# Scores of 1024 users against 100,001 items on one core: chunks of 4096 items instead of 2048, with longer rows in stores and loads

## The chip, the cores and the metric

The kernel runs on one core of one Trainium2 chip. The metric is the device time of one execution in microseconds (us); medians of several runs are quoted. PE is TensorE, DVE is VectorE, ACT is ScalarE, POOL is GpSimd, and SP is SyncE, which issues the stores and loads treated here. The profile counts 16 DMA engines for the core. The chips that the runs fell on differ by some 5% of this kernel's time (before takes 1645 us on two and about 1733 us on another), all of it in the first third (the rest takes 1135.4 and 1136.0 us), for a reason that stays open (see the result), so kernels are compared on the same chip, as ratios, or from one common instruction of the trace to the end.

## The reference, cut to what matters

```python
e = emb[seq]                                   # 1024 x 50 gathered rows of 128 floats
prefix = jnp.cumsum(e, axis=1)
uF = prefix / denom[:, :, None]                # then normalised over the 1024 users
...
_, spikes = lax.scan(step, v0, x_seq)          # 50 time steps
uF_out = spikes.mean(axis=0)                   # 1024 x 128
scores = uF_out @ emb.T                        # 1024 x 100001 floats: 409.6 MB written
```

The first half (the gather phase) is 50 steps of gathers and small vector work. The second (the output stage) reads the table once (51 MB), multiplies, and writes 409.6 MB. The change concerns the second and the seam between the two.

## The kernel before: the parts concerned

Item rows are fetched in chunks of 2048, 16 chunks ahead. A partition holds every 128th row, so each piece of a load is one row of 512 bytes:

```python
CH = 2048; AHEAD = 16; HALF = 1024
r = rowp.tile([P, CH // P, D], F32, ...)
nc.sync.dma_start(out=r[:, :full, :],
                  in_=table[c0 : c0 + full * P, :].rearrange("(k p) d -> p k d", p=P))
```

A "preparation" makes 1024 items ready for the products: eight transposes into PSUM, then a split into an upper part (ACT) and a lower part (DVE).

```python
for k0 in range(0, hw, P):
    nc.tensor.transpose(pt[:, k0 : k0 + kw], r[:kw, (h0 + k0) // P, :], ident[:kw, :kw])
nc.scalar.copy(hi[:, :hw], pt[:, :hw])
nc.vector.tensor_tensor(lo[:, :hw], pt[:, :hw], hi[:, :hw].bitcast(F32), ALU.subtract)
```

The output stage goes chunk by chunk, and in a chunk through eight blocks of 128 users. A block is evicted from PSUM in pieces of 1024 columns, by DVE and ACT in turn, into one of four 1 MiB buffers, and stored. The next chunk is prepared along the way:

```python
op = ctx.enter_context(tc.tile_pool(name="o", bufs=4, reuse_waits="tile"))
for c0 in range(0, N, CH):
    for n in range(NB):                        # NB = 8
        o = op.tile([P, CH], F32, tag="o", ...)
        for h0 in range(0, w, HALF):
            ...                                # four products into po
            # DVE or ACT in turn: o[:, h0:h0+hw] = po * (1/T)
        nc.sync.dma_start(out=out[n * P : (n + 1) * P, c0 : c0 + w], in_=o[:, :w])
        if n in (1, 4) and c0:
            ... prepare(nxt, h0, ...)          # one of the two halves of the next chunk
        if n == 4 and c0 + AHEAD * CH < N:
            fetch(c0 + AHEAD * CH)
```

## Time and profile before

| before | value |
|---|---|
| time, median of the first 3 runs | 1730.06 us (1729.33 to 1733.63) |
| span of the profiled execution | 1642.6 us |
| DMA rate, loads mixed in / stores only | 395 / 406 GB/s |
| score stores | 1 MiB each, rows of 8192 bytes |
| loads | 1 MiB each, pieces of 512 bytes |

The profiled execution is 87 us shorter than the timed ones. Besides the lines that the prediction quotes, these of the page of before are needed below. The groups' columns are busy time and mean ns of one, then the idle time ahead of them and what ended it.

```profile
span 1642.6 us, 14074 instructions
...
DMA packets 98817, 488.20 MB, mean 297 GB/s; under 512 B 15845, under 2 KB 17592, under 8 KB 49592
...
L92 DVE TENSOR_TENSOR lo<-pt,hi 128x1024 fp32r<-128x1024 f32 x98 | 119.7, 1221 | 76.1 <-ACT hi L91 76.1
...
L91 ACT CAST hi<-pt 128x1024 fp32r<-128x1024 f32 x98 | 98.7, 1007 | 8.0 <-PE pt L90 8.0
```

The reader is to keep two durations: the halves of the split take 1221 ns on DVE and 1007 ns on ACT. A preparation therefore keeps the two evicting engines from evicting for about as long as one piece of a block (1223 ns on DVE, 1020 ns on ACT).

### The profile page before, as it was taken

What the parts mean: (1) busy time and instruction counts of PE and PEld (TensorE: products, weight loads), DVE (VectorE), ACT (ScalarE), POOL (GpSimd) and SP (SyncE); (2) the same over time, 40 slices, a digit from 0 to 9 for tenths busy, and PEclk for the clock granted to TensorE, in tenths of its full rate; (3) what the DMA queues carried; (4) which work ended last, traced back from release to release, by engine and by line L of the source; (5) the groups of instructions that cost most, each with busy time, mean ns of one, the idle gap of its engine ahead of it and who ended that gap; (6) DMA issues with size and microseconds to landing.
All of it is one profiled execution on the core that took longest, in us unless ns stands there. A gap on an engine that the chain in (4) does not pass through costs nothing.

```text
span 1642.6 us, 14074 instructions
## 1 busy us (share of the span) xinstructions
PE 1294.6 (79%) x4621; PEld 837.6 (51%) x4634; DVE 963.5 (59%) x1258; ACT 637.1 (39%) x698; POOL 378.4 (23%) x406
## 2 busy tenths in 40 slices
PE   5777777777777778778877877887788798888886
PEld 2332232223334556656655665565566566666664
DVE  4777777777776445444544544454455455555554
ACT  2332222323333344434443444444444444444443
POOL 7777777777771000000000000000000000000000
PEclk6555555555556899999999999999999999999999
DMA  9921222221223999999999999999999999999998
GB/s 256 257 53 53 53 53 53 53 53 53 53 53 142 396 397 393 404 394 386 398 399 391 391 404 393 392 396 400 391 393 401 394 417 409 404 406 406 401 402 347
DMA packets 98817, 488.20 MB, mean 297 GB/s; under 512 B 15845, under 2 KB 17592, under 8 KB 49592
## 3 DMA queue, kind: packets, MB, share of 16 engines
q1 hardware_dynamic: 85944, 461.07, 72.1%
q0 software_dynamic: 12800, 26.24, 6.1%
q8 instruction: 36, 0.59, 0.1%
q14 instruction: 37, 0.30, 0.1%
HBM read 77.65 MB, written 409.60 MB: 297 GB/s over the span
## 4 chain that ended last, share of the span: by engine, by line
DMA 54%; POOL 16%; PE 12%; issue 8%; DVE 5%; ACT 4%; DVEq 0%; ACTq 0%; SPq 0%; POOLq 0%
DMA scores<-o 51%; POOL e L122 16%; PE po L301 10%; ACT o L311 3%; DVE o L309 3%; DMA e<-in_L_rec_emb_table,idx 3%; PE pre L179 1%; PE pt L90 1%; PE pre L219 0%; DVE s L199 0%; DVE bs L229 0%; DVE uF L228 0%; ACT v L264 0%; DVE v L267 0%; PE count L189 0%
## 5 line engine op out<-in xcount | busy, mean ns | idle before, releaser
L301 PE MATMUL po<-hi,countR 128*128 128x512 f32 x1568 | 678.0, 432 | 183.8 <-ACT o L311 180.9
L309 DVE TENSOR_SCALAR o<-po 128x1024 f32<-128x1024 f32 x392 | 479.3, 1223 | 463.6 <-DMA scores<-o 438.9
L301 PE MATMUL po<-lo,countR 128*128 128x512 f32 x1568 | 645.8, 412 | 0.0
L311 ACT ACTIVATE o<-po 128x1024 f32<-128x1024 f32 (+1 forms) x392 | 399.9, 1020 | 633.0 <-DMA scores<-o 514.3
L301 PEld LDWEIGHTS po<-hi,countR 128*128 128x128 f32 x1568 | 314.1, 200 | 336.3 <-ACT o L311 249.6
L122 POOL DMA_INDIRECT e<-in_L_rec_emb_table,idx x400 | 377.7, 944 | 124.3 <-issue 115.5
L301 PEld LDWEIGHTS po<-lo,countR 128*128 128x128 f32 x1568 | 315.0, 201 | 60.0
L219 PE MATMUL pre<-ident,e 128*128 128x128 f32 x400 | 143.0, 443 | 122.8 <-DMA e<-in_L_rec_emb_table,idx 118.7
L179 PE MATMUL pre<-zT,l 50*128 50x512 f32 x200 | 186.8, 1086 | 2.3 <-DVE uF L228 2.3
L219 PEld LDWEIGHTS pre<-ident,e 128*128 128x128 f32 x400 | 80.3, 206 | 202.1 <-DMA e<-in_L_rec_emb_table,idx 179.4
L92 DVE TENSOR_TENSOR lo<-pt,hi 128x1024 fp32r<-128x1024 f32 x98 | 119.7, 1221 | 76.1 <-ACT hi L91 76.1
L237 ACT ACTIVATE r<-mv,eps 128x1 f32<-128x1 f32 x50 | 14.7, 295 | 296.7 <-DVE mv L233 296.7
L228 DVE SCALAR_TENSOR_TENSOR uF<-rlen,pre 128x512 f32<-128x512 f32 x100 | 68.3, 683 | 95.3 <-PE pre L219 95.3
L90 PE MATMUL pt<-ident,rows 128*128 128x128 f32 x782 | 108.3, 283 | 15.6 <-ACT o L311 9.9
L90 PEld LDWEIGHTS pt<-ident,rows 128*128 128x128 f32 x782 | 89.3, 144 | 47.5 <-ACT o L311 35.3
L91 ACT CAST hi<-pt 128x1024 fp32r<-128x1024 f32 x98 | 98.7, 1007 | 8.0 <-PE pt L90 8.0
L179 PEld LDWEIGHTS pre<-zT,l 50*128 50x128 f32 x200 | 57.4, 317 | 65.3 <-issue 38.4
L264 ACT ACTIVATE v<-uF,hgb,a 128x1024 f32<-128x1024 f32 (+1 forms) x51 | 60.8, 1193 | 49.4 <-DVE a L257 49.2
L229 DVE BATCH_NORM_STATS2 bs<-uF 128x6 f32<-128x512 f32 x100 | 69.5, 695 | 3.4
L267 DVE SCALAR_TENSOR_TENSOR v<-negv,v 128x1024 f32<-128x1024 f32 (+1 forms) x51 | 61.6, 1209 | 13.0 <-ACT v L264 13.0
L199 DVE TENSOR_SCALAR s<-v 128x1024 bf16<-128x1024 f32 (+1 forms) x51 | 60.9, 1194 | 0.1
L266 DVE TENSOR_TENSOR negv<-s,v 128x1024 f32<-128x1024 bf16 x48 | 58.1, 1211 | 0.0
(41 smaller groups left out, 216.8 us busy)
## 6 DMA issues: line engine op xcount, KB each, us to landing
scores<-o SPq DMA_DIRECT2D x384, 1024.0 KB, 9.0
scores<-o SPq DMA_DIRECT2D x8, 848.5 KB, 7.4
e<-in_L_rec_emb_table,idx POOLq DMA_INDIRECT x400, 2.5
rows<-in_L_rec_emb_table SPq DMA_DIRECT2D x1, 832.0 KB
rows<-in_L_rec_emb_table SPq DMA_DIRECT2D x48, 0.5 KB, 11.7
idx<-in_r_seq SPq DMA_DIRECT2D x1, 200.0 KB, 3.0
r<-in_L_rec_emb_table SPq DMA_DIRECT2D x1, 25.0 KB
rows<-in_L_rec_emb_table SPq DMA_DIRECT2D x1, 16.5 KB
```

The costliest lines, as they stand in the source:

```text
L90: nc.tensor.transpose(pt[:, k0 : k0 + kw], r[:kw, (h0 + k0) // P, :], ident[:kw, :kw])
L91: nc.scalar.copy(hi[:, :hw], pt[:, :hw])
L92: nc.vector.tensor_tensor(lo[:, :hw], pt[:, :hw], hi[:, :hw].bitcast(F32), ALU.subtract)
L122: nc.gpsimd.indirect_dma_start(out=es[t][:, n * P : (n + 1) * P], out_offset=None, in_=table, in_offset=bass.IndirectOffsetOnAxis(ap=idx[: ...
L179: nc.tensor.matmul(pre[h], lhsT=l, rhs=zT[:, h * BANK : (h + 1) * BANK], start=t == 0, stop=False, skip_group_check=True,)
L219: nc.tensor.matmul(pre[h][:, k : k + P], lhsT=e[:, h * BANK + k : h * BANK + k + P], rhs=ident, start=False, stop=last, is_transpose=True, ...
L228: nc.vector.scalar_tensor_tensor(uF[:, cs], rlen[:, cs], 1.0 / (t + 1), pre[h], ALU.max, ALU.mult)
L229: nc.vector.bn_stats(bs[:, h, :], uF[:, cs])
L267: nc.vector.scalar_tensor_tensor(vt[:, cs], negv[:, cs], -0.5, vt[:, cs], ALU.mult, ALU.add)
L301: nc.tensor.matmul(po[:, k0 : k0 + kw], lhsT=countR[:, n * P : (n + 1) * P], rhs=part[:, k0 : k0 + kw], start=j == 0, stop=j == 1,)
L309: nc.vector.tensor_scalar_mul(o[:, h0 : h0 + hw], po[:, :hw], 1.0 / T)
L311: nc.scalar.mul(o[:, h0 : h0 + hw], po[:, :hw], 1.0 / T)
```

## The change

Its intent: fewer and longer rows for the DMA engines, in both directions, and an earlier first store. The core of the diff:

```diff
-CH = 2048
-AHEAD = 16
+CH = 4096
+AHEAD = 7
...
+            nc.sync.dma_start(           # a load: eight table rows in a row per partition, 4 KB runs
+                out=r[:, : whole * KQ, :].rearrange("p (q k) d -> p q (k d)", q=whole),
+                in_=table[c0 : c0 + whole * HALF, :].rearrange("(q p k) d -> p q (k d)", p=P, k=KQ),
+            )
...
+        return (                         # the split reads PSUM with a stride, to undo that order
+            pt.rearrange("d (k p) -> d p k", k=KQ),
+            hi.rearrange("d (p k) -> d p k", k=KQ),
+            lo.rearrange("d (p k) -> d p k", k=KQ),
+        )
...
+        x(halves[0])                     # the last time step, in halves and reordered
+        x(halves[1])
+        ...                              # the first block: five stores of 256, 256, 512, 512, 512 KB
...
-    op = ctx.enter_context(tc.tile_pool(name="o", bufs=4, reuse_waits="tile"))
+    op = ctx.enter_context(tc.tile_pool(name="o", bufs=3, reuse_waits="tile"))
...
+                if n == NB - 1 and q < 2:
+                    ready(c + 1, 2 + q)  # preparations 2 and 3 of the next chunk, inside the last block
+            if c or n > 1:
+                store(n, c0, o[:, :w])   # 2 MiB, rows of 16 KB
+            if n in (2, 5):
+                ready(c + 1, n // 5)     # preparations 0 and 1
+        if c + AHEAD < len(chunks):
+            fetch(c + AHEAD, rowp)       # 2 MiB
```

(Comments are mine; cuts are marked with "...".)

More of the change, by code (lines that the diff above doesn't have):

```diff
@@ L23 @@
 V_TH = 1.0
-CH = 2048
-AHEAD = 16
+CH = 4096
+AHEAD = 7
 HALF = 1024
+KQ = HALF // P
 BANK = 512
@@ L50, in rec_kernel @@
     const = ctx.enter_context(tc.tile_pool(name="const", bufs=1))
-    embp = ctx.enter_context(tc.tile_pool(name="embT", bufs=4))
-    rowp = ctx.enter_context(tc.tile_pool(name="rows", bufs=AHEAD))
-    countR = const.tile([P, B], F32R, tag="countR", name="countR")
+    embp = ctx.enter_context(tc.tile_pool(name="embT", bufs=1))
+    rowp = ctx.enter_context(tc.tile_pool(name="rows", bufs=AHEAD - 1))
+    countA = const.tile([P, P], F32R, tag="countA", name="countA")
+    countB = const.tile([P, BANK - P], F32R, tag="countB", name="countB")
@@ L56, in rec_kernel @@
+    countC = const.tile([P, B - BANK], F32R, tag="countC", name="countC")
+    counts = [countA]
+    counts += [countB[:, k : k + P] for k in range(0, BANK - P, P)]
+    counts += [countC[:, k : k + P] for k in range(0, B - BANK, P)]
     ident = const.tile([P, P], F32, tag="ident", name="ident")
+    chunks = [(c0, min(CH, N - c0)) for c0 in range(0, N, CH)]
     rows = {}
     split = {}
-    def fetch(c0):
-        w = min(CH, N - c0)
-        full, rest = divmod(w, P)
-        r = rowp.tile([P, CH // P, D], F32, tag="rows", name=f"rows_{c0}")
+    order = {}
@@ new lines, in rec_kernel, with fetch @@
+    for c, (c0, w) in enumerate(chunks):
+        for q in range(-(-w // HALF)):
+            order[c, q] = len(order)
+    def fetch(c, pool):
+        c0, w = chunks[c]
+        r = pool.tile([P, CH // P, D], F32, tag="rows", name=f"rows_{c}")
+        whole = w // HALF
+        if whole:
+            nc.sync.dma_start(
+                out=r[:, : whole * KQ, :].rearrange("p (q k) d -> p q (k d)", q=whole),
+                in_=table[c0 : c0 + whole * HALF, :].rearrange("(q p k) d -> p q (k d)", p=P, k=KQ),
+            )
+        c1 = c0 + whole * HALF
+        full, rest = divmod(w - whole * HALF, P)
+        k0 = whole * KQ
@@ L66, in fetch @@
         if full:
             nc.sync.dma_start(
-                out=r[:, :full, :],
-                in_=table[c0 : c0 + full * P, :].rearrange("(k p) d -> p k d", p=P),
+                out=r[:, k0 : k0 + full, :],
+                in_=table[c1 : c1 + full * P, :].rearrange("(k p) d -> p k d", p=P),
             )
         if rest:
-            nc.sync.dma_start(out=r[:rest, full, :], in_=table[c0 + full * P : c0 + w, :])
-        rows[c0] = r
-    def prepare(c0, h0, pt):
-        w = min(CH, N - c0)
-        hw = min(HALF, w - h0)
-        r = rows[c0]
-        if c0 == 0 and h0 == 0:
-            nc.vector.memset(r[0:1, 0, :], 0.0)
-        hi = embp.tile([P, HALF], F32R, tag="hi", name=f"hi_{c0}_{h0}")
-        lo = embp.tile([P, HALF], F32R, tag="lo", name=f"lo_{c0}_{h0}")
+            nc.sync.dma_start(out=r[:rest, k0 + full, :], in_=table[c1 + full * P : c0 + w, :])
@@ new lines, in fetch, with turned, slot @@
+        rows[c] = r
+    def turned(c, q, pt):
+        hw = min(HALF, chunks[c][1] - q * HALF)
+        if c == 0 and q == 0:
+            nc.vector.memset(rows[c][0:1, 0, :], 0.0)
+        for k0 in range(0, hw, P):
+            kw = min(P, hw - k0)
+            nc.tensor.transpose(pt[:, k0 : k0 + kw], rows[c][:kw, q * KQ + k0 // P, :], ident[:kw, :kw])
+    def slot(c, q):
+        i = order[c, q] % 6
+        pool = embp if i < 4 else embp2
+        hi = pool.tile([P, HALF], F32R, tag=f"hi{i}", name=f"hi_{c}_{q}")
+        lo = pool.tile([P, HALF], F32R, tag=f"lo{i}", name=f"lo_{c}_{q}")
+        split[c, q] = hi, lo
+        return hi, lo
@@ L85, in prepare, with views, upper @@
+    def views(c, q, pt, hi, lo):
+        hw = min(HALF, chunks[c][1] - q * HALF)
+        if hw < HALF:
+            return pt[:, :hw], hi[:, :hw], lo[:, :hw]
+        return (
[3 more added lines that the diff above has]
+        )
+    def upper(c, q, pt):
+        hi, lo = slot(c, q)
+        hw = min(HALF, chunks[c][1] - q * HALF)
         if hw % 2:
@@ L87, in prepare, with lower, product, store @@
             nc.vector.memset(lo[:, hw : hw + 1].bitcast(F32), 0.0)
-        for k0 in range(0, hw, P):
-            kw = min(P, hw - k0)
-            nc.tensor.transpose(pt[:, k0 : k0 + kw], r[:kw, (h0 + k0) // P, :], ident[:kw, :kw])
-        nc.scalar.copy(hi[:, :hw], pt[:, :hw])
-        nc.vector.tensor_tensor(lo[:, :hw], pt[:, :hw], hi[:, :hw].bitcast(F32), ALU.subtract)
-        split[c0, h0] = hi, lo
+        vp, vh, vl = views(c, q, pt, hi, lo)
+        nc.scalar.copy(vh, vp)
+    def lower(c, q, pt):
+        vp, vh, vl = views(c, q, pt, *split[c, q])
+        nc.vector.tensor_tensor(vl, vp, vh.bitcast(F32), ALU.subtract)
+    def prepare(c, q, pt):
+        turned(c, q, pt)
+        upper(c, q, pt)
+        lower(c, q, pt)
+    def product(po, c, q, n, k0, kw):
+        kw += kw % 2
+        for j, part in enumerate(split[c, q]):
+            nc.tensor.matmul(
+                po[:, :kw],
+                lhsT=counts[n],
+                rhs=part[:, k0 : k0 + kw],
+                start=j == 0,
+                stop=j == 1,
+            )
+    def store(n, c0, o):
+        nc.sync.dma_start(out=out[n * P : (n + 1) * P, c0 : c0 + o.shape[1]], in_=o)
     with ExitStack() as ph:
+        row0p = ph.enter_context(tc.tile_pool(name="rows0", bufs=1))
         once = ph.enter_context(tc.tile_pool(name="once", bufs=1))
+        lp = ph.enter_context(tc.tile_pool(name="lif", bufs=2))
+        sp = ph.enter_context(tc.tile_pool(name="stats", bufs=3))
+        up = ph.enter_context(tc.tile_pool(name="uF", bufs=2))
         gp = ph.enter_context(tc.tile_pool(name="gather", bufs=3))
-        up = ph.enter_context(tc.tile_pool(name="uF", bufs=2))
-        sp = ph.enter_context(tc.tile_pool(name="stats", bufs=3))
-        lp = ph.enter_context(tc.tile_pool(name="lif", bufs=2))
         accp = ph.enter_context(tc.tile_pool(name="acc", bufs=1, space=bass.MemoryType.PSUM))
@@ L113, in rec_kernel @@
         nc.sync.dma_start(out=gb[:, 1:2], in_=beta.rearrange("(d o) -> d o", o=1))
-        for c0 in range(0, min(AHEAD * CH, N), CH):
-            fetch(c0)
+        for c in range(min(AHEAD, len(chunks))):
+            fetch(c, rowp if c else row0p)
         es = {}
@@ L169, in rec_kernel, with only @@
         count = [accp.tile([P, BANK], F32, tag=f"count{h}", name=f"count{h}") for h in range(B // BANK)]
-        def row0(t):
+        def only(t):
             l = sp.tile([T, D], F32, tag="l", name=f"l_{t}")
@@ L203, in rec_kernel @@
         v = s = None
-        correct(0, row0(0))
-        l = row0(1)
+        correct(0, only(0))
+        l = only(1)
         for t in range(T):
@@ L262, in rec_kernel, with x @@
             st = lp.tile([P, B], BF16, tag="s", name=f"s_{t}")
-            for h, cs in enumerate(halves if last else [whole]):
+            def x(cs):
                 nc.scalar.activation(vt[:, cs], uF[:, cs], AF.Identity, bias=hgb[:, 1:2], scale=a)
-                if t and not last:
-                    nc.vector.tensor_tensor(negv, s, v, ALU.subtract)
-                nc.vector.scalar_tensor_tensor(vt[:, cs], negv[:, cs], -0.5, vt[:, cs], ALU.mult, ALU.add)
-                if last:
-                    spike(st, vt, cs)
-                    counted(t, st, h)
-                    for k in range(0, BANK, P):
-                        put = nc.scalar.copy if k % (2 * P) == 0 else nc.vector.tensor_copy
-                        put(countR[:, h * BANK + k : h * BANK + k + P], count[h][:, k : k + P])
@@ L274, in rec_kernel, with step @@
-            v, s = vt, st
-            if t + 2 < T:
-                l = row0(t + 2)
-            if T - 10 <= t < T - 2 and t % 2 == 0:
-                k = (t - T + 10) // 2
-                prepare(k // 2 * CH, k % 2 * HALF, vp.tile([P, HALF], F32, tag="v1", name=f"pt_{k}"))
-    op = ctx.enter_context(tc.tile_pool(name="o", bufs=4, reuse_waits="tile"))
+            def step(cs):
+                nc.vector.scalar_tensor_tensor(vt[:, cs], negv[:, cs], -0.5, vt[:, cs], ALU.mult, ALU.add)
+            if not last:
+                x(whole)
+                if t:
+                    nc.vector.tensor_tensor(negv, s, v, ALU.subtract)
+                step(whole)
+                v, s = vt, st
+                if t + 2 < T:
+                    l = only(t + 2)
+                if T - 8 <= t < T - 2 and t % 2 == 0:
+                    q = (t - T + 8) // 2
+                    prepare(0, q, vp.tile([P, HALF], F32, tag="v1", name=f"pt_{q}"))
@@ new lines, in rec_kernel @@
+        pt = vp.tile([P, HALF], F32, tag="v0", name="pt_3")
+        turned(0, 3, pt)
+        x(halves[0])
+        x(halves[1])
+        for h, cs in enumerate(halves):
+            step(cs)
+            spike(st, vt, cs)
+            if h == 0:
+                counted(T - 1, st, 0)
+                nc.scalar.copy(countA, count[0][:, :P])
+        upper(0, 3, pt)
+        o = gp.tile([P, HALF], F32, tag="e", name="o_0_0_0")
+        for h, po in enumerate(pre):
+            product(po, 0, 0, 0, h * BANK, BANK)
@@ new lines, in rec_kernel @@
+        counted(T - 1, st, 1)
+        nc.scalar.mul(o[:, :BANK], pre[0], 1.0 / T)
+        store(0, 0, o[:, :BANK])
+        lower(0, 3, pt)
+        nc.vector.tensor_scalar_mul(o[:, BANK:], pre[1], 1.0 / T)
+        store(0, BANK, o[:, BANK:])
+        nc.scalar.copy(countB, count[0][:, P:])
+        for q in range(1, 4):
+            o = (up if q == 3 else gp).tile([P, HALF], F32, tag="uF" if q == 3 else "e", name=f"o_0_0_{q}")
+            po = vp.tile([P, HALF], F32, tag=f"v{q % 2}", name=f"po_0_0_{q}")
+            for k0 in range(0, HALF, BANK):
+                product(po[:, k0 : k0 + BANK], 0, q, 0, k0, BANK)
+            for h, cs in enumerate(halves):
+                if h == 0:
+                    nc.scalar.mul(o[:, cs], po[:, cs], 1.0 / T)
+                else:
+                    nc.vector.tensor_scalar_mul(o[:, cs], po[:, cs], 1.0 / T)
+            store(0, q * HALF, o)
+            if q == 1:
+                nc.vector.tensor_copy(countC, count[1])
@@ L285, in rec_kernel @@
+    embp2 = ctx.enter_context(tc.tile_pool(name="embT2", bufs=1, reuse_waits="tile"))
+    op = ctx.enter_context(tc.tile_pool(name="o", bufs=3, reuse_waits="tile"))
     psum = ctx.enter_context(
@@ L288, in rec_kernel, with ready @@
     turn = 0
-    for c0 in range(0, N, CH):
-        w = min(CH, N - c0)
+    def ready(c, q):
+        if (c, q) in order:
+            prepare(c, q, psum.tile([P, HALF], F32, tag="ps", name=f"pt_{c}_{q}"))
+    for c, (c0, w) in enumerate(chunks):
         for n in range(NB):
-            o = op.tile([P, CH], F32, tag="o", name=f"o_{c0}_{n}")
-            for h0 in range(0, w, HALF):
+            if c == 0 and n == 0:
+                continue
+            o = op.tile([P, CH], F32, tag="o", name=f"o_{c}_{n}")
+            for q in range(-(-w // HALF)):
+                h0 = q * HALF
                 hw = min(HALF, w - h0)
-                po = psum.tile([P, HALF], F32, tag="ps", name=f"po_{c0}_{n}_{h0}")
+                po = psum.tile([P, HALF], F32, tag="ps", name=f"po_{c}_{n}_{q}")
                 for k0 in range(0, hw, BANK):
-                    kw = min(BANK, hw - k0)
-                    kw += kw % 2
-                    for j, part in enumerate(split[c0, h0]):
-                        nc.tensor.matmul(
-                            po[:, k0 : k0 + kw],
-                            lhsT=countR[:, n * P : (n + 1) * P],
-                            rhs=part[:, k0 : k0 + kw],
-                            start=j == 0,
-                            stop=j == 1,
-                        )
+                    product(po[:, k0 : k0 + BANK], c, q, n, k0, min(BANK, hw - k0))
                 if turn % 2 == 0:
@@ L312, in rec_kernel @@
                 turn += 1
-            nc.sync.dma_start(out=out[n * P : (n + 1) * P, c0 : c0 + w], in_=o[:, :w])
-            nxt = c0 + CH
-            if n in (1, 4) and c0:
-                h0 = 0 if n == 1 else HALF
-                if nxt + h0 < N:
-                    prepare(nxt, h0, psum.tile([P, HALF], F32, tag="ps", name=f"pt_{nxt}_{h0}"))
-            if n == 4 and c0 + AHEAD * CH < N:
-                fetch(c0 + AHEAD * CH)
+                if c == 0 and n == 1 and q % 2:
+                    store(n, c0 + h0 - HALF, o[:, h0 - HALF : h0 + HALF])
+                if n == NB - 1 and q < 2:
[6 more added lines that the diff above has]
+            fetch(c + AHEAD, rowp)
 _INS = ["r_seq", "r_lengths", "L0_rec_emb_table", "L0_rec_gamma", "L0_rec_beta"]
```

## The prediction

> **What bounds the kernel now.** I read the page from the top: busy shares, then the 40 slices, then the chain of waits.
>
> ```profile
> PE 1294.6 (79%) x4621; PEld 837.6 (51%) x4634; DVE 963.5 (59%) x1258; ACT 637.1 (39%) x698; POOL 378.4 (23%) x406
> ...
> DMA  9921222221223999999999999999999999999998
> GB/s 256 257 53 53 53 53 53 53 53 53 53 53 142 396 397 393 404 394 386 398 399 391 391 404 393 392 396 400 391 393 401 394 417 409 404 406 406 401 402 347
> ...
> DMA 54%; POOL 16%; PE 12%; issue 8%; DVE 5%; ACT 4%; DVEq 0%; ACTq 0%; SPq 0%; POOLq 0%
> ```
>
> There are two programs in one. Up to about 505 us the GpSimd gathers pace the 50 time steps (400 issues of 0.94 us plus 0.3 us of issue each, about 1.24 us x 400 = 497 us). From 520 us to the end the DMA row stands at 9 and the rate at 390 to 417 GB/s: 409.6 MB of scores are written and two thirds of the table is read. The busiest compute engine, PE at 79% of the span, is not what ends the chain: 54% of it is DMA. The waits say the same from the other side, both evicting engines wait for a store to free its buffer:
>
> ```profile
> ACT o L311 <- DMA scores<-o: 514.3, 310, 5.9
> DVE o L309 <- DMA scores<-o: 438.9, 277, 5.7
> ```
>
> Next, the busy time of each engine in three stretches: with loads mixed in, stores only, and the tail. Columns after the times are PE clock, DMA share and GB/s.
>
> ```profile
> 740.21:1240.00 499.79, 398.56 (x1672) 301.11 (x1671) 252.11 (x209) 209.37 (x209) 0.00 (x0) 0.93 1.01 395
> 1320.00:1600.00 280.00, 248.32 (x1074) 174.43 (x1073) 161.72 (x134) 134.48 (x135) 0.00 (x0) 1.00 0.99 406
> ```
>
> The DMA engines are full in both (1.01 and 0.99). So only what shortens the DMA work itself, or starts it earlier, moves the end. The chain in order of time gives the cadence of that work:
>
> ```profile
> 740.21 16.93 DMA scores<-o x2
> 764.07 17.03 DMA scores<-o x2
> 788.02 17.01 DMA scores<-o x2
> ...
> 1576.67 8.97 DMA scores<-o
> 1587.05 8.97 DMA scores<-o
> 1597.43 8.98 DMA scores<-o
> ```
>
> With four buffers of 1 MiB the stores-only stretch comes round every 10.38 us, 2.595 us a store. With loads, eight stores and one 1 MiB load take 23.9 us, so a load costs 23.9 - 8 x 2.595 = 3.1 us. The last lines needed are the evictions near the end, where the block narrows from 2048 to 1697 columns:
>
> ```profile
> 1611.71 1.03 ACT L311 ACTIVATE o<-po 128x1024 f32<-128x1024 f32 x1 [1.56 <-DMA scores<-o]
> 1614.30 1.02 ACT L311 ACTIVATE o<-po 128x1024 f32<-128x1024 f32 x1 [1.56 <-DMA scores<-o]
> ...
> 1628.98 0.73 ACT L311 ACTIVATE o<-po 128x673 f32<-128x673 f32 x1 [1.44 <-DMA scores<-o]
> 1631.14 0.73 ACT L311 ACTIVATE o<-po 128x673 f32<-128x673 f32 x1 [1.43 <-DMA scores<-o]
> ```
>
> They show 2.59 us per store with 8192-byte rows and 2.16 us with 6788-byte rows.
>
> [...]
>
> **The change, part by part.**
>
> 1. Stores of 16 KB rows instead of 8 KB. Of the score stores, 190 become 2 MiB (24 full chunks x 8, less two blocks at the start), each in place of two. The saving per pair is one DMA's fixed cost. Three readings of it:
>  - Cadence: 2.595 - 2.163 = 0.432 us for 8 rows x 1404 bytes an engine, 38.5 ps a byte; 8 x 8192 bytes then cost 2.52 us, leaving about 0.08 us fixed.
>  - The trace's packet records: 8192-byte packets average 317.1 ns in the stores-only stretch, 6788-byte ones 267.4 ns. The slope is 35.4 ps a byte, leaving 27 ns a packet, times 8, plus a 9 ns completion write: 0.23 us.
>  - [...]
>  I choose 0.13 us. 190 x 0.13 = 25 us, all on the path that sets the end, since the DMA share is 0.99 or more.
>
> 2. Loads of 4 KB runs (eight rows in a row per partition) instead of 512-byte runs. In the mixed stretch the packet records show 2048-byte load packets of four rows at 102 ns, 25.5 ns a row; at 36 ps a byte the bytes of a row are 18.4 ns, so 7 ns a row are overhead. A 4096-byte run should take 4096 x 0.036 + 7 to 27 = 154 to 174 ns, against 204 for the same bytes now. Per 2 MiB an engine has 32 of them, about 5.25 us against 6.53. What the wall pays is less, because loads overlap stores a little: 3.1 of 3.27 us per MiB now. Scaled alike, 5.0 us per 2 MiB load. Before: 32 full loads in the output stage x 3.1 = 99 us. After: 7 chunks of 4096 are fetched ahead instead of 16 of 2048, 4096 rows (2.1 MB) fewer, so 17 full loads x 5.0 = 85 us. Saved 14 us. The initial fetch also becomes cheaper, but the gathers are paced by GpSimd, so that is hidden.
>
> 3. The last step and the first block. Before, the first store goes out late:
>
> ```profile
> 519.99 8.45 SPq L313 DMA_DIRECT2D scores<-o  x5
> ```
>
>  From the timeline, the last statistics end at 507.5, the first counts at 511.8 and the first product at 514.9. After: both ACT halves run first, the counts of the first 128 users are copied at about 512.1 (0.27 us), four products at the slow clock take 1.9 us (0.43 us each and a lead-in), the first half is evicted by about 514 and 256 KB go out. I place the pieces at 514.0 (0.25 MiB), 515.2 (0.25), 517.4 (0.5), 519.2 (0.5) and 521 (0.5). By 521 the DMA has done 1.5 MiB where before it had 0.4. That is 2.8 us ahead, minus gaps of about 1 us until the first 2 MiB block at 528. I count 3 us because the clock should also rise earlier.
>
> 4. Strided PSUM reads in the split into upper and lower parts: 98 each on ACT (1007 ns) and DVE (1221 ns). If they doubled, DVE would gain 120 us over 1120, on an engine about half busy in this stage. Off the path.
>
> 5. Three output buffers of 2 MiB instead of four of 1 MiB. A buffer's round is landing, eviction (two of 1.23 us on DVE beside two of 1.02 us on ACT, about 2.7 us), issue, transfer 5.05 us[...]: 9.8 us, against 3 x 5.05 = 15.2 us of cadence. The queue does not run dry. The built instruction order agrees: the load of the next chunk waits for transposes that are already done.
>
> Sum: 25 + 14 + 3 = 42 us. Timed runs of before stand at 1730 us and the profiled one at 1643. I cannot tell from one profile where those 87 us lie, so I carry the 42 us over unscaled: 1688. I take 1690, a little on the careful side.
>
> **The rivals.**
>
> - The rate of the stores is a limit of bytes, not of pieces. For it: [...]the cadence reading gives only 0.08 us fixed, uncertain by as much again. Then part 1 gives 5 to 10 us and the sum is 25: 1705, "same".
> - The larger fixed cost of the packet records is right: 0.23 us x 190 = 44 us, sum 61: 1669.
> - PE becomes the bound. A 2 MiB block needs 16 products, 0.227 us apart at full clock in the timeline, 3.6 us, plus half a preparation (eight transposes in 1.1 us, so 0.5 us): 4.15 us at full clock, 4.5 at 0.93, against 5.05 of DMA. It holds, but a 5 us load idles PE longer than a 3 us one, and at half clock 8.3 us exceeds the DMA. If the clock fell much below 0.82 the gain would go: about 1725. The queue of two 2 MiB stores (10 us) speaks against it[...].
> - Three buffers run dry around loads or in the tail of 848 KB stores (round 5.6 us against 6.5 of cadence, close). Cost 5 to 10 us: about 1697.
>
> **Range and chances.** The first two rivals span 1669 to 1705; adding the dry queue or the unexplained 87 us scaling with the stores (42 x 1730 / 1643 = 44) gives 1668 to 1714 for 8 in 10. The line for faster is 1695.5, just above my number: 0.58 faster, 0.40 same, 0.02 slower.
>
> **What would show each step.** Step 1: stores-only rate of 412 to 418 GB/s instead of 406, and packets of 16384 bytes at about 610 to 620 ns; at 632 or more the step is wrong. Step 2: load packets of 4096 bytes at 154 to 174 ns, and a mixed rate of 408 or more instead of 395. Step 3: first score store near 514 us. Step 4: the split instructions at 1.0 and 1.2 us, or longer without harm. Step 5: DMA share still 0.99 or more between stores. I am wrong in kind if the share falls below that while ACT and DVE wait for PE, or if timed and profiled differences between the kernels disagree by more than a few us.

What no trace or run of this case shows is cut from the recorded text, and each cut is marked: a paragraph of hardware notes, the third reading in part 1, the figure for the landing in part 5, and a clause each in the first and the third rival. The sum came to 25 + 14 + 3 = 42 us. But the 0.13 us behind the 25 had been chosen with the cut reading beside the two that stand, so take it as the author's estimate: with 0.08 or 0.23 us it would be 15 or 44 us. In part 5 the round came to 9.8 us: 2.7 for eviction and 5.05 for transfer, and the other 2.05 were the estimate of the landing.

## The result, and the profile after

| | before | after |
|---|---|---|
| time, median of 4 runs | 1731.71 us (1729.33 to 1733.63) | 1702.64 us (1702.28 to 1706.29) |

The ratio is 0.9838, with a 95% interval of 0.9817 to 0.9858. Ratios here are the mean time of one kernel's fast runs over that of the other's fast runs of the same rounds, so not quite the ratio of the medians quoted. By the 2% line this is "same"; it is 29 us gained where 42 had been added up.

The page of the changed kernel: span, DMA share and rate in 40 slices, chain, packets, and the two halves of the split.

```profile
span 1701.1 us, 13009 instructions
...
DMA  9211111111111089999999999999999999999998
GB/s 348 95 45 45 47 48 47 43 48 48 47 44 47 22 344 408 424 422 409 410 401 407 401 407 402 405 410 411 402 402 406 401 400 397 425 416 415 419 415 346
DMA packets 58329, 488.12 MB, mean 287 GB/s; under 512 B 12485, under 2 KB 13208, under 8 KB 33688
...
DMA 43%; DVE 22%; PE 15%; another core or an unknown queue 10%; ACT 6%; issue 3%; POOL 0%; SPq 0%; ACTq 0%; DVEq 0%; POOLq 0%
...
L134 DVE TENSOR_TENSOR lo<-pt,hi 128x1024 fp32r<-128x1024 f32 x98 | 117.3, 1217 | 50.6 <-ACT hi L130 45.8
...
L130 ACT CAST hi<-pt 128x1024 fp32r<-128x1024 f32 x98 | 99.0, 1011 | 45.3 <-PE pt L101 40.3
```

Three things are to be seen. The packets fell from 98817 to 58329 for the same bytes. The strided reads of PSUM cost nothing (1217 and 1011 ns, against 1221 and 1007). And the span is 58.5 us *longer* than the profiled one of before, while the timed runs are 29 us shorter. The gather phase explains that: the output stage starts only in slice 15 of 40, where before it was full in slice 14 of a shorter span, and the chain names "another core or an unknown queue" for 10%. The table of waits of the changed kernel (engine, what it waited for, total us, times, longest) shows where:

```profile
ACT o L411 <- DMA scores<-o: 376.1, 133, 8.9
DVE o L409 <- DMA scores<-o: 351.9, 129, 7.7
DVE uF L291 <- remote: 172.0, 19, 20.6
...
POOL e L185 <- remote: 64.3, 16, 4.5
```

In the gather phase there are 16 to 19 waits, of 9 us on average on DVE and 4 on GpSimd, that the first profile of before does not have and that the profile puts down to nothing in the program ("remote"). The code of the gathers is the same in both kernels. Either the change brought these waits, or the two profiles come from different chips. To keep them apart from the rest, I read the time of the last statistics (the last instruction of the gather phase that both kernels share) in the vector engine's timeline, of before:

```profile
507.26 0.21 DVE L233 BATCH_NORM_AGGREGATE mv<-bs 128x2 f32<-128x12 f32 x1
```

and of after:

```profile
591.69 0.21 DVE L296 BATCH_NORM_AGGREGATE mv<-bs 128x2 f32<-128x12 f32 x1
```

From there to the end of the span before took 1642.6 - 507.3 = 1135.4 us, after 1701.1 - 591.7 = 1109.4 us (such differences are taken before rounding): 26 us shorter. The stretches of after, with loads mixed in and with stores only (columns: stretch, us, busy time of PE, PEld, DVE, ACT and POOL, granted clock, DMA share, GB/s), stand against those of before in the prediction (395 and 406 GB/s):

```profile
740.00:1340.00 600.00, 466.60 (x2060) 366.46 (x2059) 304.50 (x258) 255.29 (x258) 0.00 (x0) 0.92 0.99 406
1450.00:1655.00 205.00, 175.25 (x813) 136.59 (x812) 119.73 (x102) 100.10 (x102) 0.00 (x0) 1.00 0.99 417
```

And the cadence in the stores-only stretch, from the chain in order of time (start us, us, what); every third store releases the buffer:

```profile
1446.98 12.60 DMA scores<-o
...
1462.12 12.66 DMA scores<-o
...
1477.33 12.65 DMA scores<-o
```

Three stores take 15.14 to 15.21 us, so 5.06 us a store, against 2 x 2.595 = 5.19 us for the same bytes before. That is the 0.13 us that the prediction chose for its first step. For the loads, SyncE's timeline is the view to read:

```profile
868.35 43.60 SPq L155 DMA_DIRECT2D scores<-o  x8
912.05 0.39 SPq L79 DMA_DIRECT2D rows<-in_L_rec_emb_table  x1
914.85 43.64 SPq L155 DMA_DIRECT2D scores<-o  x8
958.58 0.39 SPq L79 DMA_DIRECT2D rows<-in_L_rec_emb_table  x1
```

From load to load it is 46.5 us. Eight stores at 5.06 are 40.5, so a 2 MiB load costs 6.1 us and not the 5.0 of the prediction; before it was 2 x 3.15 = 6.3 for as many bytes. So the first step is there and the second is not. The theory from here, A: *the stores' gain is whole, and the loads' gain is lost in a hole in the DMA work once per chunk*. Rivals: B, the longer stores brought less and the loads more than thought; C, the gather-phase waits are the change's doing and hide part of the gain; D, loads of 4 KB runs are simply no faster beside stores.

### The profile page after: what moved, and what is told of

The parts are those of the page before. It is cut to its first block, busy times and chain, and to the rows that moved or that the text cites. A ratio compares the mean times of both kernels' runs of the same rounds, so it can differ in the third digit from the quotient of the medians.

```text
span 1701.1 us, 13009 instructions
## 1 busy us (share of the span) xinstructions
PE 1206.4 (71%) x4621; PEld 844.5 (50%) x4634; DVE 947.9 (56%) x1257; ACT 631.4 (37%) x698; POOL 378.4 (22%) x406
## 2 busy tenths in 40 slices
DMA packets 58329, 488.12 MB, mean 287 GB/s; under 512 B 12485, under 2 KB 13208, under 8 KB 33688
## 4 chain that ended last, share of the span: by engine, by line
DMA 43%; DVE 22%; PE 15%; another core or an unknown queue 10%; ACT 6%; issue 3%; POOL 0%; SPq 0%; ACTq 0%; DVEq 0%; POOLq 0%
DMA scores<-o 42%; PE po L146 14%; ACT o L411 4%; DVE bs L292 4%; DVE uF L291 4%; DVE v L331 3%; DVE s L262 3%; DVE negv L336 2%; DVE o L409 2%; ACT v L328 1%; DMA e<-in_L_rec_emb_table,idx 1%; DVE mv L296 1%; PE pt L101 1%; DVE a L320 1%
## 5 line engine op out<-in xcount | busy, mean ns | idle before, releaser
L409 DVE TENSOR_SCALAR o<-po 128x1024 f32<-128x1024 f32 x390 | 463.1, 1220 | 473.9 <-DMA scores<-o 351.9
L146 PE MATMUL po<-hi,countC 128*128 128x512 f32 x784 | 343.1, 438 | 155.0 <-ACT o L411 154.9
L146 PE MATMUL po<-lo,countC 128*128 128x512 f32 x784 | 327.0, 418 | 0.0
L146 PEld LDWEIGHTS po<-hi,countC 128*128 128x128 f32 x784 | 162.1, 207 | 215.2 <-ACT o L411 182.4
L146 PE MATMUL po<-hi,countB 128*128 128x512 f32 x588 | 234.7, 399 | 22.1 <-ACT o L411 22.1
L146 PE MATMUL po<-lo,countB 128*128 128x512 f32 x588 | 229.6, 391 | 0.0
L146 PEld LDWEIGHTS po<-lo,countC 128*128 128x128 f32 x784 | 162.3, 207 | 31.9
L134 DVE TENSOR_TENSOR lo<-pt,hi 128x1024 fp32r<-128x1024 f32 x98 | 117.3, 1217 | 50.6 <-ACT hi L130 45.8
L146 PEld LDWEIGHTS po<-hi,countB 128*128 128x128 f32 x588 | 110.9, 189 | 54.3 <-ACT o L411 32.2
L146 PEld LDWEIGHTS po<-lo,countB 128*128 128x128 f32 x588 | 111.1, 189 | 21.8
L130 ACT CAST hi<-pt 128x1024 fp32r<-128x1024 f32 x98 | 99.0, 1011 | 45.3 <-PE pt L101 40.3
L282 PE MATMUL pre<-ident,e 128*128 128x128 f32 x400 | 99.5, 423 | 14.0 <-DMA e<-in_L_rec_emb_table,idx 10.4
```

The source lines that it names most:

```text
L130: nc.scalar.copy(vh, vp)
L134: nc.vector.tensor_tensor(vl, vp, vh.bitcast(F32), ALU.subtract)
L146: nc.tensor.matmul(po[:, :kw], lhsT=counts[n], rhs=part[:, k0 : k0 + kw], start=j == 0, stop=j == 1,)
L282: nc.tensor.matmul(pre[h][:, k : k + P], lhsT=e[:, h * BANK + k : h * BANK + k + P], rhs=ident, start=False, stop=last, is_transpose=True, ...
L409: nc.vector.tensor_scalar_mul(o[:, h0 : h0 + hw], po[:, :hw], 1.0 / T)
```

## The experiments

Twelve runs were made, in three calls. All of one call fell on one chip, with runs of before beside them: 1733.66 us (first call), 1645.44 us (second), 1644.63 us (third).

### 1. Before again, unchanged

No edit. 

> The kernel before once more, for a second profile: its timed runs are 1730 us but the profile in hand spans 1643 us. Theory A: the 87 us lie in the gather phase, as in the profile of the changed kernel (all engines idle for about 11 us once every 34 us); then this profile spans about 1730, the last statistics end near 590 us instead of 507, and from there to the end it is 1134 us as in the first profile. Rival: the timed runs write more slowly; then the gather phase ends near 507 again and the stores-only rate is about 375 GB/s.

Measured: 1735.36 us. The span, the waits and the last statistics of its profile on this chip are:

```profile
span 1733.4 us, 14074 instructions
```

```profile
DVE uF L228 <- remote: 152.1, 14, 20.2
...
POOL e L122 <- remote: 72.0, 16, 7.6
```

```profile
597.49 0.21 DVE L233 BATCH_NORM_AGGREGATE mv<-bs 128x2 f32<-128x12 f32 x1
```

The old kernel has the same "remote" waits here. Its last statistics come 90 us later than in its first profile, and from there to the end it takes 1733.4 - 597.5 = 1136.0 us, against 1135.4. So the 87 us between profile and timed runs lie in the gather phase, belong to the chip (or to its state) and not to the kernel, and do not touch the output stage. Rival C falls. From here on, "from the last statistics to the end" is the measure for single profiles: before 1136, after 1109.

### 2. The changed kernel with loads in 512-byte pieces

```diff
-        whole = w // HALF
+        whole = 0
...
-        if hw < HALF:
+        if True:                      # no strided views: the order is the old one
             return pt[:, :hw], hi[:, :hw], lo[:, :hw]
```

> The changed kernel with its loads in the old layout (512-byte rows), all else kept. Theory: the 4 KB runs bought almost nothing on the wall (6.1 us per 2 MiB against 2 x 3.15), so about 1706 us (1702 to 1710). The prediction's step 2 says 17 loads x (6.2 - 5.0) = 20 us slower: 1722.

Measured: 1713.49 us, ratio to before 0.9883 (0.9865 to 0.99), so 11 us slower than after (1702.6), and 1118.6 us from the last statistics to the end, 9 more than after. The 4 KB runs do save something. Their number lay between what my theory and the prediction had said, which is a hint that two things were mixed; the third experiment and the fifth take them apart.

### 3. The changed kernel with rows of 8 KB in the stores

```diff
-                store(n, c0, o[:, :w])
+                for s0 in range(0, w, CH // 2):
+                    store(n, c0 + s0, o[:, s0 : min(s0 + CH // 2, w)])
```

> The changed kernel with every 2 MiB block sent as two stores of 8 KB rows, both issued when the block is ready. Theory: the fixed cost of a store and its rows returns, 190 x 0.13 = 25 us: 1727 us, packets of 8192 bytes at 317 ns. Rival (row length does not matter, the gain came from elsewhere): 1703.

Measured: 1709.86 us, ratio 0.986 (0.9842 to 0.9877): only 7 us slower than after, not 25. A miss. The stretches of this kernel:

```profile
740.00:1340.00 600.00, 469.34 (x2068) 367.90 (x2066) 304.66 (x259) 256.22 (x259) 0.00 (x0) 0.93 1.01 408
1450.00:1655.00 205.00, 171.12 (x789) 133.44 (x788) 117.34 (x100) 98.55 (x100) 0.00 (x0) 0.99 0.99 406
```

With stores only it is back at before's 406 GB/s, as it should be. With loads mixed in it is *no slower* than after (408 against 406), though its rows are shorter. From load to load it takes 46.46 us; eight blocks are 8 x 5.19 = 41.5, so a load costs 4.95 us. That is the prediction's 5.0, and it means that the 6.1 of after are not what the load needs: something in after's mixed stretch is lost that this kernel does not lose. In the trace, the first half of a chunk's last block leaves 3.8 us ahead of the load, where after's whole block leaves 0.4 us ahead of it. The half did not have to wait for what stands ahead of the whole.

### 4. The changed kernel without loads in the output stage (wrong)

```diff
-            fetch(c + AHEAD, rowp)
+            rows[c + AHEAD] = rows[c + 1]      # old rows used again: wrong scores
```

> The changed kernel without the 18 loads of the output stage (it uses old rows again, so the scores are wrong on purpose). Theory: the loads cost 17 x 6.1 us and 2.5 us for the last, so about 1597 us. If a load cost 5.0 us as predicted and the rest was lost in dry buffers or PE, about 1615 us.

Measured: 1598.99 us, ratio 0.9229 (0.921 to 0.9248), with a relative error of 1.19, as was meant. From the last statistics to the end 1004.2 us: the loads cost after 1109.4 - 1004.2 = 105.2 us.

### 5. The two preparations moved behind the last block's store

The trace of after around a last block, on the vector engine:

```profile
906.94 1.23 DVE L409 TENSOR_SCALAR o<-po 128x1024 f32<-128x1024 f32 x1 [2.73 <-DMA scores<-o]
908.08 2.35 DVE L134 TENSOR_TENSOR lo<-pt,hi 128x1024 fp32r<-128x1024 f32 x2
910.34 1.22 DVE L409 TENSOR_SCALAR o<-po 128x1024 f32<-128x1024 f32 x1
```

The buffer is released at 906.9; then eviction, two halves of a split, eviction; and the store is issued at 911.6, 4.7 us after the release. A block without preparations needs half of that. The edit:

```diff
-                if n == NB - 1 and q < 2:
-                    ready(c + 1, 2 + q)
             if c or n > 1:
                 store(n, c0, o[:, :w])
             if n in (2, 5):
                 ready(c + 1, n // 5)
+            if n == NB - 1:
+                ready(c + 1, 2)
+                ready(c + 1, 3)
```

> The changed kernel with the two preparations that stood inside a chunk's last block moved behind its store. Theory: in the mixed stretch the changed kernel is not limited by DMA but by its buffers: the last block's store comes 2.2 us later than it could (four DVE instructions of 1.22 us instead of two ahead of it), the DMA engines run dry for about 0.65 us a chunk just then (measured from the packets), and the 8 x 0.13 = 1.0 us a chunk that the 16 KB rows save is lost there. Then the chunk period falls from 46.56 to about 45.5 to 45.9 us and the time by 11 to 17 us, to 1686 to 1692. Rival (a load simply costs 6.1 us beside 16 KB stores, whatever the buffers do): 1702.

Measured: 1605.93 us (1605.51 to 1608.25) on a chip where before takes 1645.44: ratio 0.9765 (0.9751 to 0.9778). The absolute numbers expected were for the other chip; after itself takes 1618.27 on such a chip (experiment 9), so this is 12 us less than after, inside the expected 11 to 17. By the 2% line it is faster than before; the 0.7% by which it is faster than after rests on a comparison of two calls, each with before beside it. From the last statistics to the end it takes 1096.3 us, 13.1 less than after. The last block of a chunk, and the stretches:

```profile
819.56 2.35 DVE L409 TENSOR_SCALAR o<-po 128x1024 f32<-128x1024 f32 x2 [2.76 <-PE po L146]
822.79 2.36 DVE L134 TENSOR_TENSOR lo<-pt,hi 128x1024 fp32r<-128x1024 f32 x2 [0.88 <-ACT hi L130]
```

```profile
640.00:1240.00 600.00, 478.18 (x2103) 373.13 (x2102) 311.40 (x264) 259.51 (x264) 0.00 (x0) 0.93 1.00 415
1350.00:1560.00 210.00, 180.95 (x828) 139.55 (x826) 120.14 (x102) 100.05 (x103) 0.00 (x0) 0.99 0.99 418
```

The two evictions now follow each other in 2.35 us and the split comes behind them. The rate with loads rises from 406 to 415 GB/s; the stores-only stretch, which has no loads to suffer, stays where it was. At a load the DMA engines no longer run dry. I laid the packets of 13 chunks over each other, counted from the issue of the load: after has a DMA share of 0.70 and 0.45 in the two half-microseconds around the issue, and lacks 0.53 us per chunk in all to a full share (the expectation had 0.65); x_late lacks 0.17, none of it at the load, x_store8 0.05, x_rows512 0.06, before 0.02.

### 6. Experiment 5 with rows of 8 KB

The edit is that of 3 on top of that of 5. 

> The same with every block sent as two stores of 8 KB rows. With the dry spot gone the row length should show in the whole stage: 190 x 0.13 = 25 us slower than the run before, against the 7 us that the same edit cost on the changed kernel. Rival (16 KB stores make loads dearer and so gain only in the stores-only stretch): 7 us slower.

Measured: 1625.38 us, ratio 0.9877 (0.9862 to 0.9892): 19 us slower than x_late. Once there is no hole to hide in, most of the 25 us of step 1 shows: it had been missing from experiment 3 only because its half stores closed the hole at the same time (19.4 lost by the rows, 12.3 won back by the hole, as 1618.27 - 1605.93 of experiments 9 and 5: 7.1, measured 7.2).

### 7. Four output buffers, one chunk less ahead

```diff
-AHEAD = 7
+AHEAD = 6
...
-    op = ctx.enter_context(tc.tile_pool(name="o", bufs=3, reuse_waits="tile"))
+    op = ctx.enter_context(tc.tile_pool(name="o", bufs=4, reuse_waits="tile"))
```

> The changed kernel with four output buffers of 2 MiB and 6 chunks fetched ahead instead of 7, so one more 2 MiB load in the output stage (5 to 6 us). Theory (buffers run dry): period 45.5, minus 17 us, plus 5.5: 1690. Rival (loads cost 6.1 us anyway): 1702 + 6 = 1708.

Measured: 1609.79 us, ratio 0.9784 (0.9769 to 0.9799), 8 us under after although it loads one chunk more in the output stage (about 5 us, an estimate from the 4.95 us of a load in experiment 3); 45.7 us from load to load, like x_late. A second way to close the same hole, without touching the order of the preparations.

### 8. Two gather buffers

```diff
-        gp = ph.enter_context(tc.tile_pool(name="gather", bufs=3))
+        gp = ph.enter_context(tc.tile_pool(name="gather", bufs=2))
```

> The changed kernel with two gather buffers instead of three. In the timed runs of both kernels all engines but GpSimd idle for about 11 us in every 34 us of the gather phase, and the wait ends some 4 us after GpSimd has filled its three buffers and stopped. If the wait can only end once GpSimd stops, two buffers shorten each wait by a time step's gathers (10 us) and the gather phase falls well below 590 us (to 520 to 560). If it is tied to a clock of 34 us, the phase stays near 590 us or grows. An open question, no firm theory.

Measured: 1616.97 us, ratio 0.9828 (0.981 to 0.9846), last statistics at 507.9. The run fell on a chip that has no "remote" waits at all, so it says nothing about them: inconclusive.

### 9. After again, on a chip without those waits

No edit. 

> The changed kernel once more, on whatever chip this is. The saving lies after the gather phase (26.6 us from the last statistics to the end, 1136.0 against 1109.4), so it should be the same 26 to 29 us on a chip whose gather phase has the waits (1733 against 1706) and on one without (1645 against 1617).

Measured: 1618.27 us (1616.61 to 1618.64) against 1644.63, ratio 0.9836 (0.9823 to 0.985); last statistics at 507.1 and 1109.4 us from there to the end, the same as on the other chip. What the change is worth does not depend on the waits.

### 10. The first block's five stores held back

```diff
-        store(0, 0, o[:, :BANK])
+        held = [(0, o[:, :BANK])]
...                                   # likewise for the other four
+        for c0, part in held:
+            store(0, c0, part)
```

> The changed kernel with the five stores of the first block held until all its pieces are ready. If storing in pieces is worth what step 3 says, 3 us slower than the changed kernel on the same chip (2 to 5); if the reordered last step alone gives the start, no difference.

Measured: 1618.95 us, ratio 0.9847 (0.9833 to 0.986), the same as after. A failed experiment: SyncE has nothing but these stores in its queue there, in the same order, so moving the calls changed nothing that runs (the first 0.25 MiB landed 9.26 us after the last statistics in both). How much of the early start is due to the pieces and how much to the reordered last step was not told apart.

### 11. Experiment 5 with each load cut into four

Besides the edit of experiment 5 (the new function `fetch_part` is left out):

```diff
-        if c + AHEAD < len(chunks):
-            fetch(c + AHEAD, rowp)
+            if c and c + AHEAD - 1 < len(chunks) and n % 2 == 0:
+                fetch_part(c + AHEAD - 1, n // 2)      # 512 KB behind every second block
```

> The kernel with the preparations behind the last store, and each 2 MiB load cut into four loads of 512 KB spread over the chunk (4 KB rows kept). If what is left of a load's cost is in the burst (slow packets at its end, one engine behind for 3 us), it gets faster by 5 to 10 us than that kernel (39.5 us under the kernel before on the same chip). If it is in the change from storing to loading (the last store packet before a load takes 1208 instead of 604 ns on 13 of 16 engines, 0.5 us), four changes a chunk cost 17 x 1.5 = 25 us more.

Measured: 1623.92 us, ratio 0.9877 (0.9861 to 0.9892), 18 us slower than x_late. The packets of the loads became faster (mean 165 ns against 178 in x_late), which the theory of a burst had promised, and it did not help. What grew is the number of slow store packets. A store packet of 16 KB most often takes 611 ns (no packet has the expectation's 604). The packets do not name their engine, so engines are counted here by packets, one each. The one just ahead of a load takes 1208 on about 13 of the 16 engines in after (9 to 13 such packets a load, most often 13), and 1208 or 1258 on about 6 in x_late. Here there are four times as many loads, and it is slow on about 10 engines for each. In 600 us the store packets of over 1100 ns cost each engine 20 us more than ordinary ones would, against 3.6 in x_late. By these counts, changing from stores to a load has a price of its own in this kernel.

### 12. Before without loads in the output stage (wrong)

```diff
-                fetch(c0 + AHEAD * CH)
+                rows[c0 + AHEAD * CH] = rows[c0 + CH]
```

> The kernel before without the loads of its output stage (wrong on purpose). By its cadence a 1 MiB load costs 23.91 - 8 x 2.595 = 3.15 us; 32 of them and 3 us for the rest are 104 us under the kernel before. If the loads were hidden beside the stores, less than 50.

Measured: 1540.78 us, ratio 0.9368 (0.9353 to 0.9382), 104 us under before (relative error 1.16, as meant). Its span and that of experiment 4 (the second on the chip with waits):

```profile
core 0: 1539.1 us, clock 0.971
```

```profile
core 0: 1596.3 us, clock 0.829
```

From the last statistics to the end it is 1031.7 us. This completes the ledger, all in us from the last statistics to the end:

| | before | after | x_late |
|---|---|---|---|
| whole | 1136.0 | 1109.4 | 1096.3 |
| without loads | 1031.7 | 1004.2 | (not run) |
| cost of the loads | 104.3 | 105.2 | |

Without loads the change saves 27.5 us; the loads cost 0.9 us more than before instead of 14 less; and moving two preparations brings 13.1 back. Rival B (the stores brought less) falls by the second line. D (4 KB runs are no faster) falls by experiment 2, where 512-byte pieces took 9 us more than after although that kernel has no hole to pay for (0.06 us a chunk).

## Why the prediction was right or wrong

The number, 1690, was 12.6 us too low, inside its range of 1668 to 1714. The class that it held likelier, faster at 0.58, did not come. Step by step:

**Step 1, stores of 16 KB rows: right in kind and size.** Predicted 0.13 us a pair, 25 us in all. Measured 5.19 - 5.06 = 0.13 us, 417 GB/s (predicted 412 to 418), and 16384-byte packets of 620 ns in the stores-only stretch (predicted 610 to 620). A packet of 8192 bytes averages 317 ns in before's, so two take 634: the pair saves 14 ns, times eight, plus 9 ns for the 4-byte packet that each engine moves once a store (the prediction's completion write), 0.12 us. That the size came out so closely is in part luck: 0.13 was chosen between readings of 0.08 and 0.23 us. The 0.23 of the second rival falls with the cadence. The first rival, a pure limit of bytes (1705), had nearly the right total for the wrong reason: this fixed part is real. Experiment 6 shows 19 us of it directly.

**Step 3, start of the output stage: right.** Predicted 3 us. The first 4 MiB were out 21.5 us after the last statistics, before 24.1: 2.6 us. The prediction placed the first store near 514 us; on a chip without the waits it was issued at 514.7. The clock rose earlier too, as the prediction had counted on: the granted clock goes from 0.5 to 1.0 at 520.4 us in before, 13.2 us after the last statistics, and at 602.3 us in after, 10.6 us after them; the products, 0.43 us apart until then, follow each other in 0.23. Steps 1 and 3 together were put at 28 us, and the ledger has 27.5.

**Step 4, strided reads of PSUM: right**, and not even the doubling that was allowed for: 1217 and 1011 ns.

**PE as the bound (the third rival): it did not come.** On one chip, two executions of after with granted clocks of 0.804 and 0.936 took 1617.5 and 1618.3 us.

**The 87 us that could not be explained: rightly carried over unscaled.** They lie in the gather phase and are the chip's. They also set off a sign of being wrong in kind, timed and profiled differences that disagree (29 us less against 58.5 more), though nothing in the mechanism was wrong there.

**Step 5, "the queue does not run dry": this is the step that failed**, and with it the fourth rival (three buffers run dry around loads, 1697) came true at 13 us instead of its 5 to 10. The prediction made the round of a buffer 9.8 us against a cadence of 15.2. Two terms of that sum were mis-sized.

First, "eviction, about 2.7 us". That holds for most blocks. In the last block of a chunk two preparations stand ahead of the store: 4.7 us from release to issue. The sign set for this step, a DMA share of 0.99 or more, could not catch it: the mixed stretch of after has 0.99, because 0.53 us in 46.5 hardly moves an average. The prediction looked at whether a *load* waits for the transposes and not at what a preparation does to the block around it.

Second, the landing, which the 9.8 us had at about 2 us, the author's estimate. The trace has 16 updates of a store's semaphore. They do not name their engine; I read them as one report from each of the 16 engines, which their number suggests. One group, a store of after, as the times of the 16 reports in us from the span's start:

```
902.71 902.72 902.72 902.77 902.82 902.84 902.84 902.88
902.89 902.89 902.90 902.94 903.04 903.48 904.91 906.82
```

Thirteen engines are done within 0.33 us, and the last is 4 us behind. The eviction that waits for this store starts at 906.92, 0.1 us after the last report and 4 us after the middle one: the buffer came free with the last. In the median of after's mixed stretch the last engine reports 3.8 us behind the middle one (4.5 with stores only). This is no fixed delay. Between loads the last reports follow each other at 5.06 us, which is the cadence of the stores, and the middle ones at 4.92, so the lag grows from 3.7 us after a load to 4.5 ahead of the next; with four buffers (x_o4) it is 7.9 us (9.4 with stores only). So when a buffer comes free, most engines are already most of a store further on than the release tells (3.8 us of the 4.92 between their stores).

Put together for the middle engine: release to issue 4.7 us, issue to first packet 0.86 us (read at the first store of the stage), its own 4.92 us between stores, and the lag of 3.8 us, make 14.3 us, and the report, about 0.5 us behind an engine's last packet, 14.8; the three buffers last 3 x 4.92 = 14.8 us. Nothing is left, where the prediction had 5.4 us to spare. Ahead of the load issued at 912.05 the store of the last block went out at 911.62 and could begin at 912.48, when the middle engine had been done with the store in front since 912.17. In the median of 13 chunks the last store goes out 0.9 us before the middle engine's report of the store in front; in x_late it is 2.3 us. What comes of it, as mean times between reports of the middle and of the last engine (12 or 13 chunks each, us):

```
                    other stores   last store of the chunk   the load behind it
middle, after           4.93               6.24                    5.89
middle, x_late          4.95               5.58                    5.36
middle, x_rows512       4.92               5.72                    6.88
last, after             5.05               5.01                    6.32
last, x_late            5.07               4.87                    5.37
last, x_o4              5.05               5.24                    5.09
```

By the middle engine the last store and its load together take 1.19 us more in after than in x_late, and the seven other stores 0.2 less. From the issue of the first full load to that of the last, 17 rounds, after takes 791.4 us and x_late 778.4: these 13.0 us are all of the 13.1 by which the ends differ.

The hole is not all of the mechanism. It accounts for 0.53 - 0.17 = 0.36 us a chunk, 6 us in all. The rest lies in slower packets: those of a load average 186 ns in after and 178 in x_late (32 of them, 0.25 us a chunk), and store packets of over 1100 ns cost 7.5 us more than ordinary ones in 600 us against 3.6 (0.3 us a chunk). And the last engine did not run dry at all: its last store takes 5.01 us, like its others, and only its load is longer, 6.32 against 5.37 us. So it is shown, by x_late and by x_o4, that buffers that come back too late around the load cost the 13 us; that the hole in the other engines is what makes the last engine's load longer is not shown.

In x_late the last store still takes 0.63 us more than the others. The doubled packet ahead of a load, about 0.6 us more on some 6 of the 16 engines, is part of that, and no kernel here has removed it.

**Step 2, loads of 4 KB runs: right as a duration, not collected.** The packets of 4096 bytes have a median of 159 ns (predicted 154 to 174). The load takes 5.36 us in x_late against 6.88 in 512-byte pieces (predicted 5.25 against 6.53 of engine time), and 4.95 us of the wall in x_store8 (predicted 5.0). But its sign, a mixed rate of 408 or more, did not come in after (406). The mean packet is 186 ns there, because about 9% of them, nearly all 3 to 6 us after the first of a 2 MiB load, take 230 ns and more; and with the hole of step 5 beside it, a load cost the wall 6.1 us. The sum of 14 us became -0.9. With the hole closed (x_late) the whole change is worth 1645.44 - 1605.93 = 39.5 us, against the 42 that were added up.

**What stays open.** What the "remote" waits of the gather phase are, which cost about 87 us on some chips. Why one engine lags behind the others, why the packets at the end of a long load are slow, and why the last engine's load is shorter once the others do not run dry. Why x_rows512 has no hole with the preparations where after has them (its last store goes out 2.4 us before the middle report, as in x_late). Why the store packet ahead of a load takes twice its time. How the early start splits between pieces and reordering.

## What to carry to other kernels

When buffers become fewer and larger, add up the round of the *worst* block, not of the usual one: what else do the evicting engines do between the release of its buffer and its store? In that sum, count from the last of the 16 engines' reports, because the others run ahead by the lag (3.8 us here) and have less work left than the number of queued stores suggests. And work that is not needed at once belongs behind the store and not ahead of it: moving two calls was worth 13 us here, as much as the new layout of all the loads had been meant to bring.
